# A hub's degree copied behind the last y pair, a weight difference kept in the last quarter's tile, and lists that begin two products sooner

## The chip, the cores and the metric

The kernel runs on one core of one Trainium2 chip, in float32. The metric is the device time of one execution in microseconds. A profile is one execution taken by the hardware profiler; its span runs from the first to the last recorded instruction. PE is TensorE (PEld its weight loads), DVE VectorE, ACT ScalarE, POOL GpSimd, and SP the engine whose queue issues most direct DMAs.

## The reference

Two layers on 2708 rows of 1024 features, with a sparse 0/1 adjacency matrix `adj` (2708 x 2708): masked attention, then a graph convolution, each with a residual and a layer norm.

```python
# layer 0
q = x @ W_q.T + b_q ; k = x @ W_k.T + b_k ; v = x @ W_v.T + b_v
z = (q @ k.T) / sqrt(1024) * adj
z = where(z == 0, -10000, z)
x = layernorm(x + relu(softmax(z, axis=1) @ v))
# layer 1
x = layernorm(x + (adj @ (x @ weight) + bias))
```

## The kernel before

The sparse path never forms the full score matrix. It takes from each row of `adj` a list of its nonzero columns (at most 24, kept in order of degree in 22 blocks of 128 records), gathers those rows of x, and works on them. A flag at the end would start a dense path, which this input does not use.

**The weight product M.** Scores need only `M`, the product of the two projection weights, so that `y = x M` replaces q and k. M is held as four quarters `m00`, `m01`, `m10`, `m11` (each 128 x 4 x 512, in the code `m_q[i][j]`, tags `m0` to `m3` of the pool `wm`). It is made by a seven-multiplication scheme: 28 half products of four matmuls each (`product_of_m`, which calls `half_products`), whose operands are differences and sums of weights: `w12 - w11`, `m_t2 = w22 - w12` (L779), `w11 <- m_t2 - w11` (L791), `w21 <- w21 - m_t2` (L792) on DVE, `s_a` and `s_b` on POOL. `m_t2` is an operand of products 9 to 12. ACT copies first parts out of PSUM (L786, L795, L802, L815); DVE adds the others on (`add`, L330, at high priority). The last four products write `m10`, tag `m2`. The PSUM pools are small: `p_o` has four banks, `p_tr` three, so product 8 needs the bank of product 5, and with it the first L330.

**What lies where.** Before M, the tags `m0` to `m3` hold `wq_i` (the loaded query weights) and a pool `wk` holds `wk_i` (the key weights). POOL multiplies `wk_i` by a bias row (L298) and ACT sums it (L299), eight times. Then `wk` is released, and the pool `mt` takes its space: `s_a`, `s_b` and, last, `m_t2`. The pool `xa`, with the x tiles `xt`, comes into the same space later.

**The y pairs and y blocks.** `y_pair` makes y for blocks 0 to 7 two by two with the same scheme (seven half products, `pair_products`; operands `t1` to `t4` are differences of quarters, `y_sums` are sums of x tiles from POOL, L403 to L406). Three of the seven results are added by DVE (L330 with `yo`); the last product of a pair waits for one of these adds, because it goes on in the same bank. `y_block` (L388) makes the rest one by one. After them come the value projection in pairs with attention, the norm, and layer 1.

**The lists.** `load_adj` brings one block of 128 adjacency rows into one of three buffers `a0` to `a2`, in six pieces. `list_columns` runs on DVE: six index searches (L239), then sorting the 48 results (L243 to L247). `count_columns` runs on ACT (L253) and then calls `load_adj` for the block three further on. Twelve lists are interleaved with M (`EARLY = 12`), ten with the y pairs. After block 9's list `sort_begin(0)` starts the sort of the first eight blocks by degree; `sort_end(0)` follows within the first y pair, and `records_out` scatters the sorted records to DRAM by POOL (L715), from where tables and records are read back.

**The hub.** The 32 rows of highest degree are cut into quarters. `deal_hub` is a generator whose steps are called by hand between and within the y pairs. Its first step gathers the records of these rows, `rec_r` (L464). The second computes `hub_i` from them (L534, tied to a matmul of pair 2) and gathers the rows' quarters. Two later steps take the nonzero columns out and sum them. The step behind the last pair computes places and copies the degree out of `rec_r` into `deg_r` (L580) for a consistency test (`full`, `bad`).

**What sets the order.** A scheduler places every engine's instructions at build time, by dependencies, its own cost estimates and priorities; on the chip each queue is then worked through in that order. `follow(later, earlier)` adds a dependency by hand, so that an instruction neither is placed nor starts ahead of another. `began` holds the first matmul of each half product so far, `products` the last matmuls of pairs and blocks, `between` functions to be called behind a given half product.

Of the kernel before, what the change touches and what calls it, by code (L numbers as in the profile page):

```python
# [9 lines left out]
F32 = mybir.dt.float32  # L10
# [11 lines left out]
P = 128  # L22
# [3 lines left out]
HALF = 512  # L26
# [16 lines left out]
EARLY = 12  # L43
# [3 lines left out]
ROW, DEG, OFF = 24, 25, 26  # L47
# [3 lines left out]
def kernel(  # L51
# [26 lines left out]


    flag = sparse_part(ctx, tc, x, xT, adj, wqT, wkT, wvT, bq, bk, bv, w1, b1, out)  # L80
    with tc.If(flag > 0):
        dense_part(tc, x, xT, adj, adjT, wqT, wkT, wvT, bq, bk, bv, w1, b1, out)


def sparse_part(ctx, tc, x, xT, adj, wqT, wkT, wvT, bq, bk, bv, w1, b1, out):
    nc = tc.nc
    N, D = x.shape
    DC = D // P
    NH = D // HALF
# [24 lines left out]
    with es:  # L114
# [3 lines left out]
        wm_pool = tc.alloc_tile_pool(name="wm", bufs=1, side="right", reuse_waits="tile")  # L118
# [88 lines left out]
        loaded, sorted_, products, applied, began, between = [], [], [], [], [], {}  # L207
# [24 lines left out]
        def list_columns(behind=None):  # L232
            b = listed[0]
            listed[0] += 1
            n, a = rows[b], loaded[b]

            at = lists.tile([P, RANGES, 8], U16, name="at_a", bufs=2)
            for i in range(RANGES):
                put = nc.vector.max_index(at[:n, i], ones[:n, :8], a[:n, cuts[i] + 8 * i:cuts[i + 1] + 8 * i + 8])  # L239
                if i == 0 and behind is not None:  # L240
                    follow(put, behind)
            few = lists.tile([P, 8 * RANGES], F32, name="few", bufs=2)
            nc.vector.tensor_tensor(few.rearrange("p (i k) -> p i k", k=8)[:n], ends[:n], at[:n], op=ALU.subtract)  # L243
            for i in range(0, KEYS, 8):
                nc.vector.max(keys[:n, b, i:i + 8], few[:n])
                if i + 8 < KEYS:
                    nc.vector.match_replace(few[:n], keys[:n, b, i:i + 8], few[:n], 0.0)  # L247

        def count_columns(behind):
            b = counted[0]  # L250
            counted[0] += 1
            n = rows[b]
            put = nc.scalar.activation(junk[:n], loaded[b][:n, :AW].bitcast(U32), AF.Sign, accum_out=cnt[:n, b:b + 1])  # L253
            follow(put, behind)
            load_adj()
# [5 lines left out]
        def follow(later, earlier, same=False):  # L261

            kind = mybir.DependencyClass.NoSync if same else mybir.DependencyClass.Sync
            tc.add_manual_dep(later.ins, earlier.ins.name, mybir.DependencyInfo(kind, mybir.DependencyReason.DATA),
                              reason="an engine's queue shall not stand still for a transfer")
# [31 lines left out]
        for c in (*range(2, DC), 0, 1):  # L297
            nc.gpsimd.tensor_tensor(wk_i[:, c, :], wk_i[:, c, :], bq_bc, op=ALU.mult)  # L298
            put = nc.scalar.activation(junk[:, :D], wk_i[:, c, :], AF.Copy, accum_out=y_col[:, c:c + 1])  # L299
# [4 lines left out]
        mt = tc.alloc_tile_pool(name="mt", bufs=1, side="right", reuse_waits="tile")  # L304
        load_adj()
        def half_products(acc, a, w, start=True, stop=True):
            for k in range(DC // 2):
                put = nc.tensor.matmul(acc, a[:, k], w[:, k], start=start and k == 0, stop=stop and k == DC // 2 - 1,  # L308
                                       skip_group_check=True)
                if k == 0:  # L310
                    began.append(put)
            for put_behind in between.pop(len(began), []):
                put_behind(put)
            return put
# [148 lines left out]
        def gather_at(src, at, n, dst, op=ALU.bypass, behind=None):  # L463
            put = nc.gpsimd.indirect_dma_start(out=dst[:n], out_offset=None, in_=src,  # L464
                                               in_offset=bass.IndirectOffsetOnAxis(ap=at, axis=0), compute_op=op)
            if behind is not None:
                follow(put, behind)
            return dst
# [33 lines left out]
        def deal_hub():  # L502
# [5 lines left out]
            def small(name, n=1, dt=F32):  # L508
                return xa.tile([P, n], dt, name=name, bufs=1)
# [22 lines left out]
            rec = gather_at(tab_ds[0][:, :], r_i, P, small("rec_r", REC, I32))  # L532
            yield
            put = nc.vector.tensor_scalar(hub_i, rec[:, ROW:ROW + 1], float(G), g_col, op0=ALU.mult, op1=ALU.add)  # L534
# [5 lines left out]
            put = nc.vector.scalar_tensor_tensor(a0, a0, 1.0, num_k, op0=ALU.is_equal, op1=ALU.mult)  # L540
# [36 lines left out]

            nc.vector.tensor_scalar(bad, mm[:, P:P + 1], float(P * HUB_SLOTS), None, op0=ALU.is_gt)
            deg_r = small("deg_r")
            nc.vector.tensor_copy(deg_r, rec[:, DEG:DEG + 1])  # L580
            full = small("full")
            nc.vector.tensor_scalar(full, deg_r, 5000.0, -10000.0, op0=ALU.is_ge, op1=ALU.mult)
            nc.vector.tensor_add(deg_r, deg_r, full)
# [45 lines left out]
            put = nc.vector.tensor_reduce(found, found_g[:, :, :HUB_SLOTS].rearrange("p g j -> p j g"), AX.X, ALU.add)  # L629
# [112 lines left out]
        def records_back(f, behind=None):  # L742
            b0, nb = families[f]
            bs, js = slice(b0, b0 + nb), slice(0, max(SLOTS[max(b0, 1):b0 + nb]))
            if f == 0:
# [8 lines left out]

        m_q = [[wm_pool.tile([P, DC // 2, HALF], F32, name=f"m{i}{j}", tag=f"m{2 * i + j}") for j in range(NH)]
               for i in range(2)]
        done, worked = 0, 0

        def product_of_m(acc, a, w, start, stop):
            nonlocal done, worked
            put = half_products(acc, a, w, start, stop)
            worked += 1
            if counted[0] < done:
                count_columns(put)
            while done < EARLY * worked // (7 * DC // 2):
                list_columns(put)
                done += 1
                if done == FAMILY + 1:  # L770
                    sort_begin(0)
# [2 lines left out]
        (w11, w12), (w21, w22) = wk_o  # L774
        A = [[(wq_of(i)[:, :DC // 2], wq_of(i)[:, DC // 2:]) for i in (c, c + DC // 2)] for c in half]
        s_a, s_b = [[mt.tile([P, DC // 2, P], F32, name=f"{n}{c}") for c in half] for n in ("s_a", "s_b")]
        m_t2 = mt.tile([P, DC // 2, HALF], F32, name="m_t2")
        nc.vector.tensor_sub(w12, w12, w11)
        nc.vector.tensor_sub(m_t2, w22, w12)  # L779
        for c in half:  # L780
# [3 lines left out]
        for c in half:  # L784
            product_of_m(pa[c], A[c][0][0], w11, True, False)
            nc.scalar.copy(m_q[0][0][:, c], pa[c])  # L786
        for c in half:
            pb = spare_bank()
            product_of_m(pb, A[c][0][1], w21, True, True)
            add(m_q[0][0][:, c], pb, m_q[0][0][:, c])  # L790
        nc.vector.tensor_sub(w11, m_t2, w11)  # L791
        nc.vector.tensor_sub(w21, w21, m_t2)  # L792
        for c in half:
            product_of_m(pa[c], s_b[c], m_t2, False, False)
            nc.scalar.copy(m_q[0][1][:, c], pa[c])  # L795
            nc.gpsimd.tensor_tensor(s_b[c], A[c][0][1], s_b[c], op=ALU.subtract)
# [13 lines left out]
        t1, t2 = [wv_pool.tile([P, DC // 2, HALF], F32, name=f"y_t{k}", tag=f"v{k - 1}") for k in (1, 2)]  # L810
        nc.vector.tensor_sub(t1, m_q[0][1], m_q[0][0])
        nc.vector.tensor_sub(t2, m_q[1][1], t1)
        for c in half:
            product_of_m(pa[c], A[c][1][1], w21, False, True)
            nc.scalar.copy(m_q[1][0][:, c], pa[c])  # L815
# [29 lines left out]
        y_sums_of(0)  # L845
        yos = [xa.tile([P, D], F32, name=f"yo{k}", bufs=1) for k in range(3)]
        deal = deal_hub()

        def load_wv(cs):
# [662 lines left out]
        for k in range(WARM):  # L1512
            put = nc.tensor.matmul(warm, ident, y_bc[:, :HALF], start=True, stop=True, skip_group_check=True)
# [353 lines left out]
```

## Time and profile before

| | us |
|---|---|
| median of three runs | 1039.7 (1037.43 to 1044.81) |
| profiled execution | 1038.42 |
| its span | 1036.6 |
| PE busy | 961.8 (93%) |
| DVE busy | 828.0 (80%) |
| POOL busy | 578.1 (56%) |
| ACT busy | 423.8 (41%) |
| mean granted clock of TensorE | 0.975 |

PE's busy time is that of its matmul records, which overlap a little; a matmul of 128 x 512 in float32 is recorded as two rows. In a timeline a row gives the start, the length, engine, source line, operation, output and inputs, the count, and in brackets how long the engine had been idle before it and what ended that. In a list of waits a row gives who waited for whom, the total, the number of times and the longest. A wait for several semaphores is put down to the one that came last.

### The profile page before, as it was taken

The numbers are of one execution on the slowest core, as the hardware profiler recorded it, in microseconds if no ns is written. First come the engines' busy times: TensorE is split into PE (matmuls) and PEld (weight loads), VectorE is DVE, ScalarE is ACT, GpSimd is POOL, SyncE is SP. The second block draws the span as 40 slices with busy tenths as digits, with TensorE's granted clock in tenths as the row PEclk, the third lists the DMA queues.
The fourth block names the chain that finished last, engine by engine and source line by source line (L and its number), as shares of the span: only waits on it lengthen the run. The fifth ranks groups of instructions, "written<-read, shape, count | busy, mean of one in ns | idle before, by whom it ended". The sixth has DMA issues, their size and how long they took to land.

```text
span 1036.6 us, 10406 instructions
## 1 busy us (share of the span) xinstructions
PE 961.8 (93%) x2723; PEld 453.7 (44%) x2723; DVE 828.0 (80%) x1979; ACT 423.8 (41%) x932; POOL 578.1 (56%) x455
## 2 busy tenths in 40 slices
PE   7999989799999999897999999997899999989994
PEld 6434434344444444444554444443444444535441
DVE  8897994995768864999999999996569877879632
ACT  4624456364534435134343445422322333352721
POOL 3851225204667742356847677682578888768510
PEclk9989999899999999998999999998999999999997
DMA  9455875748989873254837878798697699987731
GB/s 354 153 166 183 247 240 160 235 158 280 235 250 329 264 222 104 99 155 140 259 109 208 262 232 258 259 276 313 196 309 207 227 302 296 335 249 207 206 115 44
DMA packets 103068, 229.20 MB, mean 221 GB/s; under 512 B 19684, under 2 KB 47084, under 8 KB 103000
## 3 DMA queue, kind: packets, MB, share of 16 engines
q0 software_dynamic: 51152, 159.04, 50.1%
q1 hardware_dynamic: 51848, 69.41, 20.8%
q8 instruction: 23, 0.38, 0.1%
q14 instruction: 45, 0.37, 0.1%
HBM read 218.10 MB, written 33.64 MB: 243 GB/s over the span
## 4 chain that ended last, share of the span: by engine, by line
PE 45%; DVE 18%; DMA 14%; issue 11%; POOL 8%; ACT 2%; SPq 0%; POOLq 0%; DVEq 0%; ACTq 0%
PE po L308 23%; PE po L388 11%; PE tr L388 5%; PE tr L308 3%; POOL g L480 3%; DVE at_a L239 3%; DMA g<-x_d,tabs 2%; DVE junkv L1028 2%; DMA xr<-x_d,tabs 2%; DMA g<-in_x_dram,tabs 2%; POOL xr L464 2%; DVE r L1087 1%; DMA yg<-y_d,tabs 1%; DVE t L330 1%; DMA g<-x_d,tab_h 1%
## 5 line engine op out<-in xcount | busy, mean ns | idle before, releaser
L480 POOL DMA_INDIRECT g<-in_x_dram,tabs x84 | 117.3, 1397 | 77.2 <-DVE got L661 28.6
L308 PE MATMUL po<-t,s_all 128*128 128x512 f32 x320 | 146.6, 600 | 6.8 <-DVE xr L330 5.8
L388 PE MATMUL po<-m,xt 128*128 128x512 f32 x288 | 124.8, 592 | 0.0
L1463 DVE SCALAR_TENSOR_TENSOR r<-g,valid,r 128x1024 f32<-128x1024 f32 x77 | 98.1, 1279 | 13.6 <-DMA g<-x_d,tabs 11.5
L1028 DVE SCALAR_TENSOR_TENSOR junkv<-yg,g 128x1024 uint8<-128x1024 f32 x84 | 102.4, 1219 | 5.8 <-DMA yg<-y_d,tabs 3.4
L308 PEld LDWEIGHTS po<-t,s_all 128*128 128x128 f32 x320 | 60.6, 192 | 85.1 <-issue 70.5
L480 POOL DMA_INDIRECT g<-x_d,tabs x66 | 76.7, 1162 | 23.2 <-issue 13.7
L1087 DVE SCALAR_TENSOR_TENSOR r<-g,pr,r 128x1024 f32<-128x1024 f32 x64 | 81.8, 1280 | 6.4 <-ACT r L1085 5.8
L990 ACT ACTIVATE junks<-t,lnm 128x1024 uint8<-128x1024 f32 (+1 forms) x40 | 45.9, 1146 | 95.8 <-DVE lnm L988 95.7
L388 PEld LDWEIGHTS po<-m,xt 128*128 128x128 f32 x288 | 54.6, 190 | 68.2 <-issue 67.2
L239 DVE FIND_INDEX8 at_a<-ones,a 128x8 uint16<-128x234 f32 (+5 forms) x132 | 82.1, 626 | 0.0
L308 PE MATMUL po<-wv,s_all 128*128 128x512 f32 x160 | 73.5, 603 | 8.4 <-DVE t L330 6.3
L308 PE MATMUL po<-w,rT 128*128 128x512 f32 x160 | 75.1, 611 | 4.3 <-DVE t L1500 4.2
L459 ACT ACTIVATE junka<-xt 128x128 f32<-128x128 f32 x168 | 51.8, 308 | 62.8 <-PE po L308 29.4
L253 ACT ACTIVATE junk<-a 128x2756 uint8<-128x2756 uint32 (+1 forms) x22 | 55.0, 2501 | 46.5 <-issue 19.3
L948 ACT COPY rT<-tr 128x512 f32<-128x512 f32 x76 | 41.2, 588 | 79.3 <-PE tr L947 79.3
L308 PE MATMUL po<-t,rT 128*128 128x512 f32 x160 | 73.1, 599 | 0.4 <-DVE t L330 0.4
L308 PE MATMUL po<-w,s_all 128*128 128x512 f32 x160 | 72.3, 592 | 0.0
L308 PE MATMUL po<-wv,rT 128*128 128x512 f32 x160 | 71.2, 595 | 0.0
L1003 ACT ACTIVATE t<-t,nmr,rstd 128x1024 f32<-128x1024 f32 (+1 forms) x40 | 48.8, 1237 | 42.1 <-DVE nmr L1002 41.9
L388 PE MATMUL tr<-m,xt 128*128 128x512 f32 x128 | 55.6, 592 | 0.0
L934 POOL DMA_INDIRECT x_d<-t,tabs x22 | 27.1, 1234 | 46.2 <-ACT t L1003 35.5
(418 smaller groups left out, 1805.6 us busy)
## 6 DMA issues: line engine op xcount, KB each, us to landing
xt<-in_xT_dram SPq DMA_DIRECT2D x21, 512.0 KB, 6.9
y_d<-yo SPq DMA_DIRECT2D x21, 512.0 KB, 3.3
a<-in_adj_dram SPq DMA_DIRECT2D x21, 413.0 KB, 5.2
a<-in_adj_dram SPq DMA_DIRECT2D x21, 338.0 KB, 4.2
a<-in_adj_dram SPq DMA_DIRECT2D x21, 263.0 KB, 3.3
wq_i<-in_wqT_dram SPq DMA_DIRECT2D x8, 512.0 KB, 5.3
wk_i<-in_wkT_dram SPq DMA_DIRECT2D x8, 512.0 KB, 10.9
wv<-in_wvT_dram SPq DMA_DIRECT2D x16, 256.0 KB, 7.1
```

Of the source, the lines that this page charges most:

```text
L239: put = nc.vector.max_index(at[:n, i], ones[:n, :8], a[:n, cuts[i] + 8 * i:cuts[i + 1] + 8 * i + 8])
L253: put = nc.scalar.activation(junk[:n], loaded[b][:n, :AW].bitcast(U32), AF.Sign, accum_out=cnt[:n, b:b + 1])
L308: put = nc.tensor.matmul(acc, a[:, k], w[:, k], start=start and k == 0, stop=stop and k == DC // 2 - 1, skip_group_check=True)
L388: put = nc.tensor.matmul(po, xts[b][:, c, :], m_q[c // 4][h][:, c % 4], start=(c == 0), stop=(c == DC - 1))
L459: put = nc.scalar.activation(junka[:, :xt.shape[2]], xt[:, c, :], AF.Copy, accum_out=xs[:, c, b:b + 1])
L480: nc.gpsimd.indirect_dma_start(out=dst[:n], out_offset=None, in_=src, in_offset=bass.IndirectOffsetOnAxis(ap=at, axis=0), bounds_check=N - ...
L948: nc.scalar.copy(rT[:, g * 4:g * 4 + 4, :], tr)
L990: nc.scalar.activation(junks[:n], t[:n], AF.Square, bias=nm[:n], accum_out=vs[:n])
L1003: applied.append(nc.scalar.activation(t[:n], t[:n], AF.Identity, bias=nmr[:n], scale=rstd[:n]))
L1028: put = nc.vector.scalar_tensor_tensor(junkv[:n], yg[:n], scale, xg[:n], op0=ALU.mult, op1=ALU.mult, accum_out=s)
L1087: nc.vector.scalar_tensor_tensor(r[:n], xg[j][:n], pr[:n, j:j + 1], r[:n], op0=ALU.mult, op1=ALU.add)
L1463: put = nc.vector.scalar_tensor_tensor(r[:n], xg[:n], ok[:n, j:j + 1], r[:n], op0=ALU.mult, op1=ALU.add)
```

## The change

Three edits.

1. The copy of the degree out of `rec_r` (L580) gets a dependency on `products[-1]`, at that point the last matmul of the last y pair. No other instruction of that step is edited.
2. `m_t2` is made in the tile with tag `m2`, the place of the last quarter, instead of in the pool `mt`; the quarter `m10` is made as a new tile with that tag just ahead of its four products. The pool `mt` shrinks by 8 KB per partition, and its other tiles move up by as much.
3. In M a list begins when `EARLY * (worked + 2) // 28` asks for it, not `EARLY * worked // 28`, and its first index search waits for the first matmul of the product before (`began[-2]`; nothing for the first list) instead of the last matmul of the product just made. The number of lists is the same. The counts on ACT keep their rule, one for each product while there are lists without one.

```diff
-            nc.vector.tensor_copy(deg_r, rec[:, DEG:DEG + 1])
+            follow(nc.vector.tensor_copy(deg_r, rec[:, DEG:DEG + 1]), products[-1])
...
-        m_q = [[wm_pool.tile([P, DC // 2, HALF], F32, name=f"m{i}{j}", tag=f"m{2 * i + j}") for j in range(NH)]
-               for i in range(2)]
+        def m_quarter(i, j, name="m"):
+            return wm_pool.tile([P, DC // 2, HALF], F32, name=f"{name}{i}{j}", tag=f"m{2 * i + j}")
+
+        m_t2 = m_quarter(1, 0, "m_t2_")
+        m_q = [[m_quarter(0, 0), m_quarter(0, 1)], [None, m_quarter(1, 1)]]
...
-            while done < EARLY * worked // (7 * DC // 2):
-                list_columns(put)
+            while done < EARLY * (worked + 2) // (7 * DC // 2) and done < EARLY:
+                list_columns(began[-2] if worked > 1 else None)
...
-        m_t2 = mt.tile([P, DC // 2, HALF], F32, name="m_t2")
...
         nc.vector.tensor_sub(t2, m_q[1][1], t1)
+        m_q[1][0] = m_quarter(1, 0)
         for c in half:
             product_of_m(pa[c], A[c][1][1], w21, False, True)
             nc.scalar.copy(m_q[1][0][:, c], pa[c])
```

The scheduler's order moves with it. On PE and POOL the order is the same but for one swap of neighbouring sums on POOL. On DVE, the index searches ahead of the first L330 of M are 18 instead of 11 and L791 stands behind it; L779 stands behind the first search of the first list; the degree copy stands behind the last add of the last pair, and `hub_i` is the first reader of `rec_r`. On ACT counts stand one to two places sooner. On SP the first four loads of x tiles, which stood together behind the twelfth adjacency block, stand two behind the thirteenth, one behind the fourteenth and one behind the fifteenth.

## The prediction

> **What bounds the kernel now.** I read the table of windows first, then the waits of PE and of DVE up to 250 us, then the timelines of those two engines around the waits found. All three edits sit in the first 250 us: the weight product M, the four y pairs, and the adjacency lists that run on DVE meanwhile. By window (us; PE, PEld, DVE, ACT, POOL busy; granted clock; DMA share; GB/s):
>
> ```profile
> 30.00:60.00 30.00, 25.44 (x54) 10.98 (x53) 25.02 (x55) 14.92 (x22) 25.95 (x18) 0.89 0.49 150
> 60.00:130.00 70.00, 70.00 (x164) 30.62 (x163) 61.49 (x238) 29.77 (x30) 16.83 (x16) 1.00 0.65 194
> 130.00:160.30 30.30, 26.05 (x60) 11.48 (x59) 29.31 (x115) 15.16 (x42) 10.27 (x11) 0.94 0.69 224
> 160.30:195.60 35.30, 27.24 (x66) 12.18 (x65) 19.80 (x71) 16.48 (x44) 11.45 (x13) 0.90 0.65 193
> 195.60:246.80 51.20, 49.86 (x124) 22.62 (x123) 48.12 (x184) 30.53 (x85) 14.29 (x13) 1.00 0.66 215
> 246.80:402.00 155.20, 155.20 (x419) 69.02 (x418) 109.63 (x193) 66.98 (x250) 91.88 (x72) 1.00 0.81 244
> ```
>
> PE is the bound, and from 246.8 to 402 it has no gap at all. Before that it has three holes. In 160.3 to 195.6 both PE and DVE are idle (27.24 and 19.80 of 35.3): something else holds both. Who holds whom, from the waits of PE and of DVE (total, times, longest):
>
> ```profile
> PE po L308 <- DVE yo L330: 12.3, 2, 8.1
> PE tr L308 <- DVE m L330: 4.6, 1, 4.6
> PE po L308 <- DVE n_r L562: 1.3, 1, 1.3
> ...
> DVE deg_r L580 <- DMA rec_r<-tab_d,r_i: 14.3, 1, 14.3
> DVE m_t L779 <- ACT junk L299: 5.0, 1, 5.0
> ```
>
> PE's three holes end with a DVE eviction add (L330); DVE's two long ones end with a transfer and with an ACT sum. The timelines of PE and DVE join them:
>
> ```profile
> 45.80 3.40 DVE L779 TENSOR_TENSOR m_t<-wk_o,wk_o 128x2048 f32<-128x2048 f32 x1 [4.98 <-ACT junk L299]
> 53.63 0.68 DVE L330 TENSOR_TENSOR m<-tr,m 128x512 f32<-128x512 f32 x1
> 54.37 6.56 PE L308 MATMUL tr<-wk_o,wq_o 128*128 128x512 f32 x8 [4.56 <-DVE m L330]
> ...
> 155.10 5.40 PE L308 MATMUL po<-y_t,xt 128*128 128x512 f32 x8 [4.25 <-DVE yo L330]
> ...
> 175.34 0.15 DVE L580 CAST deg_r<-rec_r 128x1 f32<-128x1 int32 x1 [14.28 <-DMA rec_r<-tab_d,r_i]
> 188.43 0.67 DVE L330 TENSOR_TENSOR yo<-po,yo 128x512 f32<-128x512 f32 x1
> 189.15 5.73 PE L308 MATMUL po<-y_t,xt 128*128 128x512 f32 x8 [8.06 <-DVE yo L330]
> ```
>
> A one-element copy of 0.15 us stands 14.28 us at the head of DVE's queue. The lists behind it are late, and so is the add that frees the bank of pair 2's last product: PE waits 8.06 us. The product after each hole is also slow: 6.56, 5.40 and 5.73 us for 8 rows, which elsewhere take 3.43 (27.47 us for 64). So the holes cost 4.56 + 3.13, 4.25 + 1.97, 8.06 + 2.30 and, in pair 6, 1.3: 25.6 us in all.
>
> **What the Trainium skill says.** "TensorE: Matmul & The Clock Gate", Part 1, gives half clock after an idle window of about 3.4 us; the three slow products agree, after holes of 4.25 to 8.06 us; after pair 6's hole of 1.34 the product took 3.70. What a hole of 3 us does, the trace leaves open. The same page, under the architectural detail, calls DVE's queue strict FIFO: the 14.28 us show it. "SBUF — State Buffer", section on the two separate sides, says that a two-input DVE operation and a GpSimd operation lock each other out: the 128x2048 subtraction took 3.90 and 3.40 us beside POOL's work (L778, L779) and 2.28 alone (L791).
>
> **The change part by part.**
>
> *Weight difference in tile m2.* Before, m_t2 lay in the space of wk_i, and L779 stood at DVE's head until the last column sum of wk_i (ACT L299, over at 45.75). Tile m2 lay over wq_i, whose last DVE reader began at 26.06; after L778 and one index of the first list the difference can start at 35.1. The wait of 4.98 us goes; the operation costs 3.9 instead of 3.4, as L778 did beside POOL. The quarter m10, now a new tile there, waits for the readers of m_t2, which are through some 50 us before m10's copies (L815): nothing.
>
> *Lists sooner.* Before, lists began at products 3, 5, 7, 10 ... 28 of M, behind that product's last matmul; now at 1, 3, 5, 8 ... 26, behind the first matmul of the product before. That is four products, 13.7 us, sooner; their number stays 12. A list is six index operations and short steps, 5.2 us (98.9 to 104.1). Counts (ACT L253) and the loads they release come two products sooner. But DVE's order changes: ahead of the first add L330 there were 11 index operations, m_t2 and L791; now there are 18 and m_t2, and L791 is behind. Walking DVE's queue from 34.83: one index 0.22, m_t2 3.9, the rest of list 1 3.4, list 2 4.7, list 3 4.4 to 5.2: the add begins at 51.4 to 52.8 against 53.63. So list 3 eats nearly all the 4.98 us won. PE's hole shrinks from 4.56 to some 3 us. I keep its slow product (without it 3.1 less); gain 1.5, bounds +4.6 and, if list 3 waits for its load, -3. The other twenty products (3.43 each) have adds with at least two products' slack, so M ends at 128.0 against 129.57.
>
> *SP's queue.* The first four xt loads stood behind 12 adjacency loads (issued at 114.64); now two stand behind 13, one behind 14, one behind 15. Load 13 follows the count behind product 23: 110.9 + 2.6, issues 2.7: the first two xt are issued at 116.2 to 119.7 and landed by 127 (7 us, as before), just ahead of pair 0. Load 15 follows the count behind product 27 (127.3); the fourth xt is issued at 130 and landed near 139. Its readers, y_s1 on POOL, then end at 144 instead of 133.7, and POOL's eight record scatters, queued behind, start at 144.2 instead of 151.92: still sooner, as DVE's positions are ready at about 141.
>
> *Pair 0.* The same 89 index operations precede the add before pair 0's last product, but DVE, idle for 14.5 us between 34.8 and 154.4, now fills most of that. PE asks for the add at 145.7 and needs it by 149.1; DVE, limited by load 15 and the sort's matmuls (138.8), gets there at about 146. The hole and its slow product go: 6.2. Pair 0 ends at 128.0 + 7 x 3.43 + 0.7 = 152.8 against 160.33.
>
> *Degree copy.* It now waits for the last product of pair 6, where DVE's next reader (place, L576) waits for a matmul right behind that product anyway and stood 1.7 us: the three moved steps (0.15, 0.15, 0.16) cost at most 0.3 there, with no product waiting. In pair 2 two lists of 4.7 to 6.3 us (one short step was stretched to 3.49 beside POOL) follow the add at 160.4, so the next add falls at 170 to 173, and PE needs it by 173.4. Hole 8.06 and slow product 2.30 go: 10.4. Pair 2 ends near 177 (before 194.7). What is late next is the first reader of rec_r that is left, hub_i (L534), at about 173; rec_r lands 23.4 us after the first scatter, as before (151.92 to 175.3), at 167.6: about 5 us of margin.
>
> *Pairs 4 and 6.* DVE was full there (48.12 of 51.2), so it sets the pace: from hub_i (189.19, now about 173.5) to pair 6's last add the same work follows, 15.7 us sooner. PE alone, without its hole of 1.3 there, would come 3.7 us earlier still; that is given back. Sum: -1.5 - 6.2 - 10.4 - 1.3 + 3.7 = -15.7.
>
> *After 246.8.* The y blocks run without a gap, scores are tied to products (DVE waited 12.54 us for PE at 415.73), and POOL's first gather waited 28.6 us for DVE's got (L661), which moves with the rest. No absolute time anchors this part, so I carry all 15.7.
>
> Against the profiled execution (1038.42; span 1036.6 and 1.8 around it) this gives 1022.7; against the median of 1039.7, 1.3 higher, 1024.0.
>
> **Rivals.**
> - *hub_i takes over the wait.* If the fourth xt or the scatters come over 5 us later, DVE stands at hub_i, and pairs 4 and 6, which it paces, move back 1:1. For: it is in DVE's queue with the same transfer. Against: the margin, and that scatters start 7.7 us sooner. With 6 us of stall: 1030.
> - *The lists block M.* If adds behind more index operations wait for adjacency loads, M's hole grows to 7 us and pair 0 keeps its own: gain 10.4 - 3 - 1 = 6, 1033. For: 150 GB/s only in that window, adds in order behind lists; against: loads of list 3 landed by about 49.
> - *Absorbed.* DVE is nearly full from 450 to 680, so a sooner start could be lost there: 1038. Against: that work starts only when products release it.
> - *Slower: xt behind the adjacency loads.* SP issues in order; load 13 also needs list 10 off its buffer. If DVE finished list 10 later than the count (113.5) and the 1 us of slack behind it, every further us would delay the xt loads and pair 0. It outweighs the 15.7 only past 130; at 142, 12 over: about 1052. Against: DVE may begin list 10 at product 21 (100.6), which puts its end near 106.
>
> **How the numbers follow.** Chances: forecast (1017 to 1028) 0.66; hub_i 0.09; lists block 0.11; absorbed 0.08; slower 0.06. The range runs from all 25.6 us gone (1014) to the lists' case (1033). About 1% (10.4 us) is what can be told from no change: faster 0.78 (the forecast, hub_i's mild half, the lists' mildest), same 0.16, slower 0.06.
>
> **What would show it.** Right: no wait of deg_r or m_t above 1 us in DVE's list; no PE hole over 1 us behind yo in pairs 0 and 2; M's hole between 2 and 4 us; the first y block (L388) at about 231 instead of 246.83, and the rest of the trace the same distance earlier. Wrong: a wait hub_i <- rec_r of several us, adds (m, L330) holding PE beyond 4.6 us in M, POOL's y_s or PE waiting for xt at 128, or a y block start at 231 with an end that has not moved.

## The result and the profile after

The changed kernel takes 1032.72 us (median of 14 runs, 1026.48 to 1036.91) against 1041.24 for the kernel before in the same comparison (14 runs, 1034.99 to 1046.5). The ratio is 0.9918, 95% interval 0.9893 to 0.9943. It is faster by 8.5 us, where 15.7 had been forecast.

The profiled execution took 1035.79 (span 1034.1), 3.1 over its own median, and that of before 1038.42, 2.8 under its median. So the two profiles differ by 2.5 us only, the medians by 8.5. Places inside the span are better witnesses. The first y block starts at 237.96 instead of 246.83 (8.87 sooner). The first product on the mean's shares, L979 in the new file and L976 in the old, which ends a hole of 6.37 us (6.36 before), starts at 466.89 instead of 475.75 (8.86 sooner). Both agree with the medians. I use these two marks below. A mark is one execution's, though: with the lists alone (below) both are 12.4 us ahead of the kernel before, where the ratio gives 7.6. From 700 us on I read no gains, because single profiles part there by several us: near 814 this one is only 3.0 us ahead of before, and a kernel of the experiments that was 0.8 us behind it at the second mark (the sort's place alone) is 9.0 ahead. Two of the profiled executions below (parts 1 and 3 together; lists held) were slow ones, over 1.5% above the fastest of their kernel, and are read only up to the first y block.

The windows of the changed kernel, cut at its own stages (us; PE, PEld, DVE, ACT, POOL busy; granted clock; DMA share; GB/s): M in two parts, pair 0, pair 2, pairs 4 and 6, the y blocks.

```profile
30.00:60.00 30.00, 25.65 (x57) 11.06 (x56) 29.19 (x72) 17.51 (x24) 24.44 (x18) 0.94 0.49 153
60.00:128.70 68.70, 68.70 (x161) 30.15 (x160) 67.57 (x256) 29.10 (x29) 13.26 (x13) 1.00 0.68 205
128.70:153.30 24.60, 24.60 (x62) 11.19 (x61) 23.11 (x77) 13.32 (x40) 11.78 (x10) 1.00 0.85 254
153.30:177.30 24.00, 24.00 (x57) 10.56 (x56) 15.78 (x56) 15.80 (x42) 11.92 (x14) 1.00 0.78 221
177.30:238.00 60.70, 53.69 (x132) 24.63 (x131) 52.19 (x194) 31.27 (x86) 17.66 (x16) 0.92 0.59 198
238.00:402.00 164.00, 164.00 (x440) 72.84 (x439) 111.52 (x204) 72.60 (x274) 93.57 (x72) 1.00 0.81 244
```

Pairs 0 and 2 have no gap on PE any more. Pairs 4 and 6, which took 52.1 us before (194.7 to 246.83), now take 60.7, and PE is idle there for 7.0. The waits of the first 250 us (who waited, on whom; total, times, longest) name it:

```profile
PE po L308 <- DVE yo L330: 7.0, 1, 7.0
PE tr L308 <- DVE m L330: 4.3, 1, 4.3
DVE a L540 <- DMA a<-in_adj_dram,hub_i: 4.1, 1, 4.1
DVE deg_r L580 <- issue: 2.0, 1, 2.0
```

The waits of `deg_r` on its transfer (14.3) and of `m_t` on ACT (5.0) are gone. A new one stands in DVE's list, `a` at L540: the first step that takes the hub's columns out of the adjacency rows just gathered. The timelines of PE and DVE show how it reaches PE:

```profile
35.60 4.20 DVE L781 TENSOR_TENSOR m_t<-wk_o,wk_o 128x2048 f32<-128x2048 f32 x1
53.96 0.67 DVE L330 TENSOR_TENSOR m<-tr,m 128x512 f32<-128x512 f32 x1
54.68 5.40 PE L308 MATMUL tr<-wk_o,wq_o 128*128 128x512 f32 x8 [4.35 <-DVE m L330]
...
149.84 3.60 PE L308 MATMUL po<-y_t,xt 128*128 128x512 f32 x8
...
172.14 0.21 DVE L534 TENSOR_SCALAR hub_i<-rec_r,g_col 128x1 int32<-128x1 int32 x1
173.87 3.60 PE L308 MATMUL po<-y_t,xt 128*128 128x512 f32 x8
...
185.74 1.61 DVE L540 SCALAR_TENSOR_TENSOR a<-a,num_k 128x677 f32<-128x677 f32 x1 [4.15 <-DMA a<-in_adj_dram,hub_i]
193.76 0.67 DVE L330 TENSOR_TENSOR yo<-po,yo 128x512 f32<-128x512 f32 x1
205.22 0.68 DVE L330 TENSOR_TENSOR yo<-po,yo 128x512 f32<-128x512 f32 x1
205.96 6.57 PE L308 MATMUL po<-y_t,xt 128*128 128x512 f32 x8 [7.01 <-DVE yo L330]
```

The last products of pairs 0 and 2 (149.84, 173.87) run in 3.60 without a hole; the last product of pair 4 has one of 7.01 ahead of it and is slow itself. It waits for the add at 205.22, which stands in DVE's queue behind the hub's key steps, and these behind L540. The gather that L540 waits for is one of POOL's. POOL's queue, from the first scatter of sorted records (L715) on:

```profile
149.17 1.16 POOL L715 DMA_INDIRECT tab_d<-rec,pos_i  x1 [5.31 <-DVE yo L330]
...
163.79 1.03 POOL L464 DMA_INDIRECT rec_r<-tab_d,r_i  x1 [0.30 <-issue]
168.93 0.55 POOL L729 DMA_DIRECT2D tab<-tab_d  x1 [4.12 <-DMA tab<-tab_d]
169.47 0.50 POOL L731 DMA_DIRECT2D tab<-tab_d  x1
173.66 0.50 POOL L730 DMA_DIRECT2D tab<-tab_d  x1 [3.69 <-DMA tab<-tab_d]
174.18 1.28 POOL L403 TENSOR_TENSOR y_s<-xt 128x512 f32<-128x512 f32 x1
...
177.97 1.27 POOL L405 TENSOR_TENSOR y_s<-xt,y_s 128x512 f32<-128x512 f32 x1
179.40 1.04 POOL L464 DMA_INDIRECT a<-in_adj_dram,hub_i  x1 [0.16 <-DVE at_a L239]
```

`hub_i` is ready at 172.35. POOL then still waits to issue the last reload of `tab0` (L728 to L731 write into that one tile; L729 and L730 were released by a transfer `tab<-tab_d`, after 4.12 and 3.69 us), and pair 4's sums follow. The gather is issued at 179.40, 7.3 us after `hub_i` began. In the kernel before, the same queue looked like this:

```profile
151.92 1.16 POOL L715 DMA_INDIRECT tab_d<-rec,pos_i  x1 [18.20 <-DVE at_a L239]
...
176.18 0.50 POOL L730 DMA_DIRECT2D tab<-tab_d  x1 [1.02 <-DMA tab<-tab_d]
176.69 1.28 POOL L403 TENSOR_TENSOR y_s<-xt 128x512 f32<-128x512 f32 x1
...
180.50 1.27 POOL L405 TENSOR_TENSOR y_s<-xt,y_s 128x512 f32<-128x512 f32 x1
189.67 1.03 POOL L464 DMA_INDIRECT a<-in_adj_dram,hub_i  x1 [7.91 <-DVE keys L245]
```

There POOL was through with reloads and sums at 181.77, while DVE, late from its stand for `rec_r` (over at 175.34), still worked off the lists ahead of `hub_i`; POOL waited 7.91 us for DVE. From the first scatter to the last sum POOL needs about 30 us in both kernels (29.9 before, 30.1 after). It begins only 2.75 us sooner now, while `hub_i` comes 17.05 us sooner. That turned the order round: now DVE waits for POOL.

### The profile page after: what moved, and what is told of

It reads as the page before. It is cut to its first block, busy times and chain, and to the rows that moved or that the text cites. A ratio compares the mean times of both kernels' runs of the same rounds, so it can differ in the third digit from the quotient of the medians.

```text
span 1034.1 us, 10424 instructions
## 1 busy us (share of the span) xinstructions
PE 961.3 (93%) x2723; PEld 453.6 (44%) x2723; DVE 832.3 (80%) x1979; ACT 423.7 (41%) x932; POOL 580.4 (56%) x455
## 4 chain that ended last, share of the span: by engine, by line
PE 47%; DMA 15%; DVE 13%; issue 12%; POOL 10%; ACT 1%; POOLq 0%; SPq 0%; DVEq 0%; ACTq 0%
PE po L308 25%; PE po L388 11%; PE tr L388 5%; DMA g<-x_d,tabs 5%; POOL g L480 4%; PE tr L308 3%; POOL xr L464 2%; DMA xr<-x_d,tabs 2%; DVE junkv L1031 2%; DMA yg<-y_d,tabs 2%; POOL wk_i L298 1%; DVE r L1090 1%; DMA r<-x_d,tabs 1%; DVE r L1466 1%; DVE t L330 1%
## 5 line engine op out<-in xcount | busy, mean ns | idle before, releaser
L480 POOL DMA_INDIRECT g<-x_d,tabs x66 | 78.9, 1196 | 26.2 <-issue 13.7
```

## The experiments

Two theories for the missing 7 us. Theory 1: DVE stands at L540 for a gather that POOL issues late, and pair 4's adds stand behind it. Theory 2: the amount of DVE's work in pairs 4 and 6 sets their length, whatever the gather does (so the prediction had it). Beside them it was open what each part of the change brings by itself. Each ratio is against runs of the kernel before that were made along with it, with its 95% interval.

**Each part alone.** Part 1 is the degree copy, part 2 the tile, part 3 the lists; each kernel is the one before with that part's lines of the diff and no others.

Degree copy alone:

> The kernel before with the degree copy alone moved behind the last pair. Both theories: DVE's wait of 14.3 us is gone, pair 2's hole of 8.06 and its slow product (10.4 us) too; M's hole of 4.6 and pair 0's of 4.25 stay, so pair 2 begins at 160.3 as before and ends near 184.4. Then hub_i comes at about 179.6. Theory 1 (the next wait is the gather of the hub's adjacency rows, which stands on POOL behind the record reloads and pair 4's sums): POOL is free for it only at about 182, it lands at 188, DVE waits 1 to 3 us at L540 and pair 4 gets a hole of 2 to 5 us. Theory 2 (DVE simply has more work ahead of pair 4's adds than the products take): no wait of DVE at L540, a hole of 3 to 6 us in pair 4 all the same. First y block at 240 to 243 against 246.8; time 4 to 7 us under before.

Measured: ratio 0.9946 (0.9920 to 0.9972). Pair 2's hole is gone, M's (4.58) and pair 0's (4.30) stay, pair 4 has 0.70, the y block starts at 237.70. The gather is issued at 180.25, 1.55 us after `hub_i`, and L540 doesn't wait. Neither theory's figures for pair 4 came out (a wait of 1 to 3 us, or a hole of 3 to 6), nor the y block at 240 to 243: `hub_i` comes 6.6 us later than in the whole change, POOL's first scatter only 2.3 us later, so the gather is nearly in time.

Tile alone:

> The kernel before with the weight difference alone put into tile m2; lists and degree copy as before. DVE's wait of 5.0 us goes, only 11 searches stand ahead of the first add, which should begin near 48.8: M's hole of 4.6 and its slow product are gone (7.7 us sooner at the end of M). DVE itself is only 5 us ahead, so pair 0's hole should grow to 6 to 8 us, and the degree copy still stands for the record transfer. Theory 'M's gain is handed back in the pairs': first y block 2 to 5 us sooner than 246.8, time 2 to 5 under before. Rival 'all of it carries': 7 to 8 sooner.

Measured: 0.9910 (0.9877 to 0.9943). M's hole falls to 0.70 and its last product runs in 3.70; `deg_r` still waits 13.22 and pair 2 has a hole of 7.07; y block at 239.05, 7.8 us sooner than before. What M wins arrives there, as the rival had it; pair 0's hole did not grow to 6 to 8 us but is 3.54.

Lists alone:

> The kernel before with lists alone begun sooner; the difference stays in the old place, the degree copy too. 18 searches and the 5.0 us wait stand ahead of the first add: it begins near 58, M's hole grows to 8 or 9 us (M ends 3.5 to 5 later). Pair 0's hole of 4.25 and slow product go (6.2). The degree copy still holds DVE for 8 to 14 us, pair 2's hole stays at 5 to 8. First y block within 3 us of 246.8; time within 4 us of before. If the lists cost nothing in M, it would be 6 us under before.

Measured: 0.9927 (0.9899 to 0.9955). M's hole is 2.86, not 8 or more: the scheduler puts `m_t` further back among the lists, where it waits only 1.55 us. Pair 0's hole is gone, pair 2 keeps 4.58, pair 4 has none, and the y block starts at 234.34, 3.6 us earlier than with all three parts and 12.5 earlier than before, where I had expected 3 at most.

By their ratios the three bring 5.6, 9.4 and 7.6 us, together 22.6; the whole change brings 8.5. At the first y block it is 9.1, 7.8 and 12.5 against 8.9. The parts work against each other.

**Two parts at a time.**

> Parts 1 and 2 of the change, the lists of M left where they were. Theory 1 (what the whole change gives back in pair 4 is the hub gather, which GpSimd issues only behind the table's reloads and pair 4's sums, and for which VectorE then stands): the same constellation arises here, since VectorE has no stand left before hub_i: M's hole under 1.5 us, pair 2 without a hole, a wait of 2 to 5 us at L540, a hole of 3 to 8 us in pair 4; the first y block starts at 236 to 239, and the time is 1031 to 1035 us. Theory 2 (VectorE has too much work in pairs 4 and 6, whatever the gather does): no wait of more than 1 us at L540 is needed, the holes of pairs 4 and 6 together are 8 to 12 us, the first y block at 239 to 242, 1035 to 1039 us.

> Parts 2 and 3 of the change, the hub's degree copied where it was. Theory 1: VectorE stands for rec_r (10 to 13 us) and pair 2 has a hole of 4 to 6 us, but in that stand GpSimd ends the reloads and sums, the gather is issued within 2 us of hub_i and L540 does not wait; pair 4 without a hole over 1 us; the first y block starts at 234 to 237, no later than in the whole change, 1030 to 1034 us. Theory 2: pair 2's hole comes on top of those of pairs 4 and 6: first y block at 241 to 244, 1036 to 1040 us.

> Parts 1 and 3 of the change, m_t2 in the pool that it had before. Theory 1: against the lists alone pair 2's hole of 4.58 us and its slow product go, but hub_i comes earlier than GpSimd is through with the reloads and sums, L540 waits 2 to 5 us, and pair 4 gets a hole of 3 to 8 us: first y block at 233 to 237, no gain over the lists alone, time 1029 to 1034 us. Rival (the parts add up): no hole in pair 4, first y block at 228 to 230, time 1024 to 1027 us.

Measured: parts 1 and 2: 0.9896 (0.9867 to 0.9925); L540 waits 2.33, pair 4's hole is 2.96, just under theory 1's 3 to 8, and the y block starts at 234.81, sooner than either theory had it; in pair 0 a hole of 3.68 stays, which I had not listed. Parts 2 and 3: 0.9945 (0.9909 to 0.9981); DVE stands for `rec_r`, the gather is issued 0.5 us after `hub_i`, L540 doesn't wait and pair 4 has no hole, as theory 1 has it, but pair 2's hole (5.46, then a product of 6.74) and M's of 4.36 put the y block at 239.81, later than I had put it for theory 1 (234 to 237). Parts 1 and 3: 0.9917 (0.9887 to 0.9947); the y block starts at 238.66 (theory 1: 233 to 237), and these lines of DVE and PE show the same stand as the whole change:

```profile
185.45 1.22 DVE L540 SCALAR_TENSOR_TENSOR a<-a,num_k 128x677 f32<-128x677 f32 x1 [4.93 <-DMA a<-in_adj_dram,hub_i]
205.27 5.75 PE L308 MATMUL po<-y_t,xt 128*128 128x512 f32 x8 [8.37 <-DVE yo L330]
```

So the stand at L540 comes with the degree copy once something else has brought pairs 0 and 2 forward.

**POOL's order changed.** Pair 4's sums behind the gather:

```diff
-            if b + 2 < FAMILY:
+            if b + 2 < FAMILY and b != 2:
                 y_sums_of(b + 2)
...
             if b in (0, 2, 6):
                 next(deal)
+            if b == 2:
+                follow(y_sums_of(4), hub_rows[-1], same=True)
```

> The changed kernel with one edit: pair 4's sums on POOL are asked for behind the gather of the hub's adjacency rows (three of the four then stand behind it), so the gather is issued at about 175.5 instead of 179.4 and lands near 182. Theory 1 (that transfer, late on POOL, is what pair 4's hole of 7.0 us comes from): DVE's wait of 4.15 us at L540 falls under 1, pair 4's hole to 1 to 3 us, the slow product goes, the first y block at 231 to 233 instead of 238.0, time 4 to 7 us under the changed kernel. Theory 2 (DVE's amount of work): the wait goes, but the hole stays over 5 us and the first y block at 236 or later.

Measured: 1027.76 us, 0.9868 (0.9836 to 0.9900). The gather moves to 176.05, only 3.1 us after `hub_i`; the last reload (174.09) is still ahead of it. The hole in pair 4 shrinks to 3.40:

```profile
176.05 1.04 POOL L539 DMA_INDIRECT a<-in_adj_dram,hub_i  x1 [0.17 <-DVE at_a L239]
183.65 0.87 DVE L545 SCALAR_TENSOR_TENSOR a<-a,num_k 128x677 f32<-128x677 f32 x1 [3.52 <-DMA a<-in_adj_dram,hub_i]
203.12 5.19 PE L308 MATMUL po<-y_t,xt 128*128 128x512 f32 x8 [3.40 <-DVE yo L330]
```

The gather is issued 3.35 us sooner than in the changed kernel, but L540 starts only 2.1 us sooner. So theory 1's figures did not come out (a wait under 1, a hole of 1 to 3 without a slow product, the y block at 231 to 233; it starts at 235.94), and theory 2's hole of over 5 us did not either. The ratio is better than the 2 us of the y block explain; that stays open.

Then the other way, the reloads of `tab0` (L729 to L731) taken off POOL's queue:

```diff
-                nc.gpsimd.dma_start(out=tab0[:HUB, :J0], in_=tab_ds[0][HUB:2 * HUB, ROW - J0:ROW])
+                nc.sync.dma_start(out=tab0[:HUB, :J0], in_=tab_ds[0][HUB:2 * HUB, ROW - J0:ROW])
```

(and the same for the other two).

> The whole change, with the three reloads of parts of tab0 (L729 to L731) issued from SyncE instead of GpSimd, so that GpSimd waits for none of them ahead of pair 4's sums and the hub gather. Theory 1 (the late gather is GpSimd's two waits of 4.12 and 3.69 us and the sums of 5.1 us ahead of it): the sums run at 165 to 171, the gather is issued within 2 us of hub_i, near 173, L540 waits under 1 us, the hole of pair 4 is under 2 us; first y block at 229 to 233, time 1024 to 1029 us. Rival (the gather is late by its landing, not by its issue, or SyncE now stands for the reloads ahead of an xt tile): L540 or the sums still wait, pair 4's or pair 6's hole is over 4 us, first y block at 236 or later, time 1031 to 1035 us.

Measured: 1033.79 us, 0.9943 (0.9922 to 0.9964). L540 waits 0.86 and pair 4's hole is 0.75, as theory 1 says, but the rival was right about the price: the reloads now wait at the head of SP's queue (L729 for 10.1 us, until the scattered records are there), x tiles and adjacency loads queue behind them, POOL's sums wait 5.85 us for an x tile, and DVE stands for an adjacency load ahead of pair 2's add:

```profile
172.22 0.09 DVE L239 MATCH_VALUE_LOAD at_a<-ones,a 128x8 f32 x1 [4.70 <-DMA a<-in_adj_dram]
177.89 5.15 PE L308 MATMUL po<-y_t,xt 128*128 128x512 f32 x8 [3.85 <-DVE yo L330]
```

The wait moved to another queue, and nothing was won against the whole change.

**The stand taken from ahead of the adds.** POOL is left alone, and L540 waits for a product of pair 4 instead of the last one of pair 2, so that it is queued behind the adds:

```diff
             put = nc.vector.scalar_tensor_tensor(a0, a0, 1.0, num_k, op0=ALU.is_equal, op1=ALU.mult)
-            follow(put, products[-1])
+            follow(put, began[-3])
```

This step is called behind pair 4's sixth product, so `began[-3]` is the first matmul of the fourth; the expectation speaks of the fifth, which is what the kernels with all repairs below use (`began[-2]`).

> The whole change, and the first step of the hub's keys (L540) asked behind the fifth product of pair 4 rather than behind the last one of pair 2; the gather is issued as late as in the changed kernel, and VectorE has the same work. Theory 1 (the stand for the gather ahead of pair 4's adds): the wait at L540 goes, the hole of 7.01 us in pair 4 falls to under 2 and its last product from 6.57 to about 3.6; the first y block starts at 229 to 234 instead of 237.96, the time is 1024 to 1029 us. Theory 2 (the amount of VectorE's work): what pair 4 gains comes back as a hole in pair 6; first y block at 236 to 239, time 1031 to 1034 us.

Measured: 1027.66 us, 0.9907 (0.9878 to 0.9935). The gather is as late as before (181.94, 8.3 us after `hub_i`), DVE has the same work, and the stand is gone; PE has no hole in pair 4 and one of 0.45 in pair 6:

```profile
191.84 0.85 DVE L540 SCALAR_TENSOR_TENSOR a<-a,num_k 128x677 f32<-128x677 f32 x1
225.11 3.70 PE L308 MATMUL po<-y_t,xt 128*128 128x512 f32 x8 [0.45 <-DVE yo L330]
233.27 0.72 PE L686 MATMUL tr<-hot,lower 128*128 128x266 f32 x2 [2.29 <-DVE hot L680]
```

The first y block starts at 229.01, 8.95 us sooner than in the changed kernel. One of these is only the sort's own matmuls, which now stand behind this mark. That settles theory 1 against theory 2: the same amount of work, and 8 us less. Yet the time hardly falls against the changed kernel (0.9907 and 0.9918; that 1027.66 lies in theory 1's range is due to a kernel before of 1037.15 in this comparison). The third line shows the next thing that is late. The matmuls of the second family's counting sort (L686), queued after two matmuls (four rows) of the first y block, now wait 2.29 us for DVE's `hot` (L680). In the changed kernel they ran ahead of that block without a wait. At the second mark (L979) only 3.5 of the 9 us are left: 463.43. Of the 5.5 lost, 2.29 are this wait, about 1 the sort's own matmuls, and 1.7 the rows right behind the wait (22 in 11.30 us; with the three repairs below 22 take 9.61).

**The sort's place.** The first y block is asked ahead of that sort:

```diff
+        y_block(FAMILY)
         later_records = sort_end(1, products[-1])
...
-                (y_last if b == NB - 1 else y_block)(b)
+                if b != FAMILY:
+                    (y_last if b == NB - 1 else y_block)(b)
```

once together with the later L540, and once by itself on the changed kernel:

> The whole change, L540 behind the fifth product of pair 4, and the first y block ahead of the second family's counting sort; M's lists and GpSimd's order as in the changed kernel. Theory 1 (the stand at L540 cost the changed kernel some 9 us, of which the kernel with later keys lost most again to the sort's stand of 2.29 us in the first y block and its slow clock): M's hole of 4.35 stays, pairs 4 and 6 have no hole over 1.5 us, the first y block starts at 227 to 230 without a stand in it, the first L979 product at 458 to 461 instead of 466.89 (plus or minus 1 for M's start), the time is 1022 to 1027 us, 6 to 10 under the changed kernel (ratio 0.982 to 0.986). Rival (time won before the y blocks is lost behind them whatever is done): ratio 0.989 to 0.993, as the changed kernel and the one with later keys.

> The whole change, and only the first y block asked ahead of the second family's sort; the stand at L540 stays. In the changed kernel TensorE did not stand for the sort, so theory 1 expects nothing of it: pair 4's hole 6 to 9 us, first y block at 236 to 239 less the sort's own 1 us, time within 3 us of the changed kernel (ratio 0.989 to 0.994). Rival (the sort's place is itself worth 3 us or more): ratio under 0.988.

Measured, both together: 1022.90 us, 0.9833 (0.9802 to 0.9864); y block at 227.34, second mark at 457.16, 9.7 us ahead of the changed kernel. By itself: 1031.91 us, 0.9914 (0.9884 to 0.9944), pair 4's hole 8.11, second mark at 467.68: nothing. PE's lines in pair 4 and 6 and in the y block, first with both, then with the sort's place alone:

```profile
223.43 3.70 PE L308 MATMUL po<-y_t,xt 128*128 128x512 f32 x8 [0.35 <-DVE yo L330]
```

```profile
206.97 6.29 PE L308 MATMUL po<-y_t,xt 128*128 128x512 f32 x8 [8.11 <-DVE yo L330]
```

In the first kernel that 0.35 is the only hole of PE over 0.3 us between 60 and 240. Without the stand at L540 and with the sort out of its way, the change brings 1.67%, 17.4 us of 1041. With the sort moved in both, and in one comparison, the kernel without the stand is 9.0 us faster than the one with it (1022.90 and 1031.91). So the stand cost the changed kernel some 9 us of its time, and the sort's place is worth something only when the stand is gone.

**M's hole.** In the changed kernel the first add of M is queued behind the searches of three lists. Here the second and later lists are asked only behind the sixth product:

```diff
-            while done < EARLY * (worked + 2) // (7 * DC // 2) and done < EARLY:
+            while done < (EARLY * (worked + 2) // (7 * DC // 2) if worked > 6 else 1) and done < EARLY:
```

> The whole change, with the second and later lists of M asked only behind the sixth product (the first one at once), nothing else. Theory 1: M's hole of 4.35 us and its slow product go, everything up to pair 4 comes 6 to 7 us sooner, the gather among it, and the stand at L540 with pair 4's hole of 6 to 8 us stays as it is: first y block at 230 to 233, time 1025 to 1029 us. Theory 2 (VectorE's amount of work): the lists that move out of M come back as a larger hole in pair 0 or pair 4 (together over 11 us): first y block at 235 to 238, time 1030 to 1034 us.

Measured: 1026.35 us, 0.9871 (0.9826 to 0.9917). M's hole is 0.84 and its last product takes 3.70; the y block starts at 233.48; and the stand in pair 4 moves along unchanged, as theory 1 says:

```profile
181.71 0.87 DVE L540 SCALAR_TENSOR_TENSOR a<-a,num_k 128x677 f32<-128x677 f32 x1 [4.49 <-DMA a<-in_adj_dram,hub_i]
201.18 6.07 PE L308 MATMUL po<-y_t,xt 128*128 128x512 f32 x8 [7.98 <-DVE yo L330]
```

**All repairs.** Sums behind the gather, L540 behind the adds, lists held in M; then the same with the sort's place as well:

> The whole change with three repairs: pair 4's sums on GpSimd behind the hub gather, L540 behind the fifth product of pair 4, and in M the second and later lists asked only behind the sixth product, so that M's first add does not stand behind two lists. Theory 1: M's hole of 4.35 us and its slow product go (under 1 us), pair 4's hole under 2, pair 6's under 2; the first y block starts at 227 to 231, the time is 1018 to 1024 us. Theory 2: the lists moved back in M return as searches ahead of the adds of pairs 4 and 6; first y block at 234 to 237, time 1026 to 1030 us.

> The kernel with the three repairs (sums behind the gather, keys behind the fifth product of pair 4, lists held in M), and in addition the first y block asked ahead of the second family's counting sort, so that TensorE doesn't stand for VectorE's L685 in the middle of that block. If that stand of 2.44 us is on the path, the y blocks take 3 to 5 us less, and the time is 1017 to 1020 us against 1041 before (ratio 0.978 to 0.981). If the y blocks are limited by something behind them (the records' scatters, the sort's own chain), the ratio stays at 0.983.

Measured: 1021.60 us, 0.9832 (0.9802 to 0.9862), y block at 220.91 (theory 1: 227 to 231), with the sort's matmuls standing 2.44 us in it; and 1018.50 us, 0.9800 (0.9758 to 0.9842), y block at 221.75 without that stand, second mark at 453.35. The latter is the fastest kernel of this study, by the ratios 12 us under the changed one. The two intervals overlap, so what the sort's place adds there isn't settled; on the second mark it is 2.6 us. Of the 17 us that the former is ahead of the changed kernel at the first y block, 10.9 are left at the second mark.

The runs together (us; hole: PE's idle time ahead of pair 4's last product):

| kernel | `hub_i` | gather issued | L540 waits | hole, pair 4 | first y block |
|---|---|---|---|---|---|
| before | 189.19 | 189.67 | 0 | 0 | 246.83 |
| degree alone | 178.70 | 180.25 | 0 | 0.70 | 237.70 |
| tile alone | 181.16 | 181.64 | 0 | 0 | 239.05 |
| lists alone | 177.17 | 177.65 | 0 | 0 | 234.34 |
| degree, tile | 173.97 | 176.19 | 2.33 | 2.96 | 234.81 |
| tile, lists | 181.18 | 181.65 | 0 | 0 | 239.81 |
| degree, lists | 170.10 | 178.32 | 4.93 | 8.37 | 238.66 |
| the change | 172.14 | 179.40 | 4.15 | 7.01 | 237.96 |
| and lists held | 166.40 | 175.03 | 4.49 | 7.98 | 233.48 |
| and sums behind | 172.92 | 176.05 | 3.52 | 3.40 | 235.94 |
| and reloads on SP | 177.93 | 178.40 | 0.86 | 0.75 | 236.61 |
| and keys later | 173.61 | 181.94 | 0 | 0 | 229.01 |
| and sort's place | 172.06 | 180.09 | 4.58 | 8.11 | 237.72 |
| and keys later, sort's place | 172.03 | 177.35 | 0 | 0 | 227.34 |
| and three repairs | 166.22 | 169.03 | 0 | 0 | 220.91 |
| and three repairs, sort's place | 167.06 | 168.74 | 0 | 0 | 221.75 |

Where the gather follows `hub_i` within 1.6 us, L540 waits under 1 us and the hole is under 1; where it comes 2.2 to 8.6 us later, both are there, unless L540 is queued behind the adds ("keys later" and the three repairs).

## Why the prediction was right and wrong

- *M, -1.5:* right in reason, half of the size, and that by luck. The third list does eat what the tile won, but more of it than I had put: the hole only shrank from 4.56 to 4.35 (forecast 3), because the add began at 53.96 instead of 51.4 to 52.8. DVE came to its first search 0.54 us later than the 34.83 that I walked from, `m_t` took 4.20 rather than 3.9, and the short step `few` (L243) was stretched to 1.10 and 1.19 us in the two lists ahead of the add, where it takes 0.19 alone. M ends at 128.72 (129.57 before, forecast 128.0) because the product behind the hole took 5.40, which I had kept at 6.56; behind the same hole of 4.35 it took 5.24 to 6.35 in other runs of this kernel's variants.
- The prediction's "2.28 alone (L791)" was read wrongly: POOL's two sums at L782 ran from 50.30 to 54.84, beside it, and took 4.54 us where the next two took 2.49. There POOL was the one that was held. A subtraction of this shape with POOL idle is L824 of the kernel before, at 134.75, of 2.27 us.
- *SP's queue, scatters at 144.2:* wrong by 5 us. The fourth x tile held POOL's sums to 137.57 and they were through at 143.86, as forecast, but then POOL waited 5.31 us: DVE's positions (L701) were ready at 148.29, not at 141. The scatters began at 149.17.
- *Pair 0, -6.2:* right. The hole and the slow product are gone, and pair 2 starts at 153.27 (152.8).
- *Degree copy, -10.4 in pair 2:* right. Pair 2 ends at 177.30 (177), `hub_i` begins at 172.14 (173) without a wait. The copy itself, now at 236.82, stands 2.00 us, with no product waiting.
- *Pairs 4 and 6, +3.7:* this is the step that failed, and nearly all of the shortfall. From pair 2's end to the first y block I had 54 us; it took 60.66. The step named `hub_i` as what is late next and stopped there. What followed on `hub_i`, its gather on POOL, was taken to follow at once, because in the trace of before it did (189.19, 189.67). But there POOL was idle for 7.91 us ahead of it, thanks to the very stand that the change removes. I moved `hub_i` 16 us forward and did not ask whether POOL, with its reloads and sums, would be through by then. The forecast's own figures left no margin for it: POOL's 30 us from a first scatter at 144.2 end at about 174, and `hub_i` was put at about 173. With the first scatter at 149.17 they end at 179.24. So POOL wasn't through: hole 7.01 plus 3.1 of slow product, 10.1 us, where the forecast had 3.7 less 1.3 for pair 6.
- The reason given for +3.7, that DVE's work sets the pace there, fell too. With L540 behind the adds the same work ran to a y block at 229.01, two us ahead of the forecast, with no hole over 0.5 in the pairs.
- *"No absolute time anchors this part":* right for the changed kernel (8.87 at the y block, 8.86 at the second mark). Where the pairs end sooner still, the sort's `hot` is the next to be late; it has no fixed time either (the sort's matmuls started at 233.27 with later keys, at 227.89 with three repairs).
- *Rivals:* "`hub_i` takes over the wait" was near in kind: the scatters came 5 us late, and the wait did move to the hub's chain, one step later than I had put it. "The lists block M" and "xt behind the adjacency loads" did not happen, nor did "absorbed": the medians differ by as much as the two marks.

The gain was 8.5 instead of 15.7; the missing 7 us are the ones of pair 4. The median of 1032.72 lies outside the forecast's own band (1017 to 1028). It is inside the whole range only by luck, because that reached to 1033 for a case (the lists block M) that did not come about.

## What to carry to other kernels

When a stall is removed, go through every queue that was working while the engine stood, not only the one that the stall held: each of them had been given that time for nothing. Ask for each when its first piece of work can begin: here POOL's 30 us could begin 2.75 us sooner, and what waits for them came 17 us sooner. A wait that is zero in the trace may be zero because of the stall; look at what its producer is doing at the new time, queue entry by queue entry, POOL's DMA waits among them. And a long-latency consumer belongs in the queue behind what PE needs next: moving L540 by a few places brought the first y block 8.95 us forward, hastening its gather 2.0, though in the time the former paid only once the sort behind it had been moved as well.

## What the runs showed of the hardware

- A product can be slow after a hole shorter than I had thought. "TensorE: Matmul & The Clock Gate", Part 1, of the Trainium skill speaks of an idle window of about 3.4 us. Here eight rows (3.43 in a run of many, 3.60 to 3.70 by themselves) took 5.40 after 2.86 (lists alone) and 2.96 (parts 1 and 2). In the later part of the traces they took 5.30 after 1.73 (751.24, the changed kernel) and 5.40 after 1.92 (816.55, before), but 3.70 after 2.53 (811.85, tile alone) and 2.54 (827.38, three repairs). So the length of the hole alone doesn't decide it: in these runs every such product was slow from 2.86 us on, none below 1.73, and between them both occur. What decides there isn't shown.
- A short two-input DVE operation beside POOL's sums can take over ten times as long, and longer than one sum (1.28 us). `few` (128x48) takes 0.19 us; in the changed kernel one that began at 175.54, while POOL's four sums ran from 174.18 to 179.2, took 2.43, and in the kernel before one that began at 177.01 took 3.49. They ended at 177.97 and 180.50, to 0.01 us where the fourth sum (L405) starts, the only one that needs the result of the sum right before it. All seven such steps of over 2 us in the runs (2.43 to 3.80) end there.
- A DMA that waits for another's landing holds all of its queue: 3.69 to 4.12 us each for the reloads of `tab0` on POOL; on SP's queue a reload stood 10.1 us, and a DVE search waited 4.70 us for an adjacency load queued behind it.
- The gather of the hub's rows (128 rows of 677 numbers) took 6.3 to 7.6 us from its issue to the start of L540, in the six kernels in which L540 waited over 2 us for it.
